# One-bank jobs freed of the other bank's readers, the last two density units in turn, and a density deadline five steps later

## The chip, the cores and the metric

The kernel runs on one core of a Trainium2 chip. The metric is device time in microseconds of one execution. Its engines run side by side, each through its own instructions in the order in which the program wrote them: TensorE (PE, with its weight loads PEld), VectorE (DVE), ScalarE (ACT), GpSimd (POOL) and SyncE (SP), which issues transfers here. They wait for each other on semaphores.

## What is computed

The input `x` is 8 images of 192 channels by 64 x 64 pixels, in fp32. Two layers follow each other, each with a group norm (32 groups) ahead of it and a residual around it:

```
x = x + attention(gn(x))      # q, k: 24 channels, v: 192; prelu on each
                              # softmax over 4096 x 4096 scores, times v
x = x + density(gn(x))        # per channel, per pixel: likelihood of a bin of width 1
```

The density evaluates a small network per channel at `x - 0.5` and at `x + 0.5`: layers of 1, 3, 3, 3, 1 numbers with positive weights, and after each of the first three layers `l + tanh(f) * tanh(l)`. Its value is the absolute difference of two sigmoids, at least 1e-6.

## The kernel before

The program is written out step by step by a planner in Python that runs while the program is built. An image's queries come in 8 blocks of 512. A block takes 16 steps (`STEPS`), so an image takes 128 (`IMG`), and the stream over 8 images has 1024 steps (`last`). In each step the main loop issues:

- the score matmuls of the step to come (`scores`, L701) into the two-bank PSUM tile `sc`, and its exp on ACT (L705);
- the max matmuls of a block that is `LEAD` = 22 steps ahead (`max_step`, L644) into the two-bank tile `mx`, which has one buffer, and the reduction of it on VectorE (L648). So the max matmul of a step waits until the reduction of the step before is through;
- 8 attention matmuls (`attend`, L716) into an accumulator in one of two PSUM tiles, `turns`, of two banks each. Blocks take the two tiles alternately;
- and `work_off`, for everything else.

`work_off` first issues what is due at the step (`run_due`), then starts at most one job (`start_job`), then density operations (`density_step`), then one POOL piece of an ending (`pool_step`).

**Jobs** use the PSUM tile that the attention isn't accumulating into (`misc`), one bank of it or both. They start only in steps 3 to 14 of a block. `guest` holds the step from which each bank may be given out again: a job with a hold of h started at step t keeps its banks until t + h + 1, and a one-bank job gets the first bank that is free. One-bank jobs are: the norm's (`norm_end`: two small matmuls L391 and L404, and their readers L396 and L409 on VectorE, hold 3), the weights' (`weights`: L477 and on, readers L496 and L501), the keys' (`keys`: L544, read by two Relus on ACT, L529) and a block's maximum (`max_end`: four transposes, "turn", L668, read by the add L673 on VectorE). Two-bank jobs are queries (L573), values (L601) and a block's finish (transposes L749, then residual L758 on VectorE). Dependencies are drawn by whole tile: a write to a tile waits for all earlier readers of the tile.

At the start of an image several things meet, which the text below calls the seam: the finish of the last image's last block (step 3), the second norm of that image (steps 6 to 12, with `root` on ACT and `fourth`, L422 to L438, on VectorE), a turn (step 10), and the end of the density of the image before that. When `fourth` has run, `density(b)` appends 12 units.

**Density units.** A unit is one of two shifts (s = 0, 1) of one channel group of half an image: 23 VectorE operations on 128 x 1024 numbers (L958) with scale, linear and tanh operations on ACT between them (L926, L935, L941, L951). Up to three units are worked on, the oldest first. An operation is issued if what it needs on another engine was issued in an earlier step and enough of the 17 SBUF buffers are free, while its engine has credit. VectorE's credit grows each step by an allowance worked out from the operations left:

```
left = sum(len(u.todo["DVE"]) for u in units if u.key[0] == units[0].key[0])
rate = left * COST["DVE"] / max(1, (units[0].key[0] + 2) * IMG + 10 - t) + OTHER
```

with a cost of 1.22 and `OTHER` 0.1; what `run_due` issues for others on VectorE is deducted. So the density of image b is spread from about step 12 of image b + 1 to step 10 of image b + 2. When both units of a pair are done, `ending` follows: sum, tanh, sign, difference and mask on POOL and ACT, then `size` (L1120) and `store` (L1124), which frees the image's `xc` buffer (three of them) after the last channel group. The fetch of the next image but one into `xc` waits for that, and the finish of its first block waits for the fetch.

**After the stream** (the tail) the allowance is 4.15 a step. What is left of image 6's density runs beside the last norm; then image 7's density runs alone, in 11 of its 12 units with a layer of sums on TensorE (L899, then tanh L907 and gate L917), and its endings on VectorE and ACT (`alone`, L1102 to L1112).

Of the kernel before, what the change touches and what calls it, by code (L numbers as in the profile page):

```python
# [17 lines left out]
def kernel(  # L18
# [288 lines left out]
        scratch.append(pair)  # L307
    ready = [0, 0]

    def start_job(t):  # L310
        p = t % STEPS
        for n, (rank, make, hold, banks, cols) in enumerate(jobs):
            if stream[0] and (p < 3 or p + max(hold, 1) >= STEPS):
                continue
            at_ = [i for i in range(2) if guest[i] <= t]
            if len(at_) < banks:
                if rank < 2:
                    return
                continue
            k = [i for i in (1, 0) if ready[i] <= t and scratch[i][0].shape[1] >= cols]  # L320
            if cols and not k:
                continue
            del jobs[n]
            pm = misc()
            for i in at_[:banks]:
                guest[i] = t + hold + 1
            if cols:
                ready[k[0]] = t + 2
            parts = make(pm if banks == 2 else pm[:, at_[0], :], scratch[k[0]] if cols else None)
            for i, fn, cost, act, pe in parts:  # L330
                at(t + i, fn, cost, act, pe)
            return
# [47 lines left out]
    def norm_end(key, n, t, then=None):  # L380
# [7 lines left out]

        def mean():
            pm = cell["pm"]  # L390
            nc.tensor.matmul(pm[:, 0:2], lhsT=gavg, rhs=cell["mv"], start=True, stop=True)  # L391

        def second():
            mv, pm = cell["mv"], cell["pm"]
            res = cell["res"] = small.tile([128, 2], F32, tag="nrm", bufs=4, name=f"nrm_{nm}")
            nc.vector.tensor_copy(res, pm[:, 0:2])  # L396
            dv = cell["dv"] = small.tile([128, 2], F32, tag="dv", name=f"dv_{nm}")
            nc.vector.tensor_tensor(dv[:, 0:1], mv[:, 0:1], res[:, 0:1], ALU.subtract)
            nc.vector.tensor_tensor(dv[:, 0:1], dv[:, 0:1], dv[:, 0:1], ALU.mult)
            nc.vector.tensor_copy(dv[:, 1:2], dv[:, 0:1])  # L400

        def variance():
            pm = cell["pm"]
            nc.tensor.matmul(pm[:, 2:4], lhsT=gavg, rhs=cell["dv"], start=True, stop=True)  # L404

        def third():
            res, pm = cell["res"], cell["pm"]
            ve = cell["ve"] = small.tile([128, 1], F32, tag="ve", name=f"ve_{nm}")
            nc.vector.tensor_tensor(ve, res[:, 1:2], pm[:, 2:3], ALU.add)  # L409
            nc.vector.tensor_scalar(ve, ve, 1e-5, None, ALU.add)  # L410
            at(now[0] + 1, root, 0.0, 2.8)
            at(now[0] + 2, fourth, 1.5)
# [33 lines left out]

        def make(pm, _):
            cell["pm"] = pm
            return [
                (0, mean, 0.0, 0.0, 0.4), (1, second, 0.8, 0.0, 0.0),  # L450
                (2, variance, 0.0, 0.0, 0.4), (3, third, 0.4, 0.0, 0.0),
            ]
# [7 lines left out]
    def weights(b, then):  # L460
        res = norms[b, 0]
        cell = {}

        def scale():
            for k, src, n in (("q", w1r, 2), ("k", w2r, 1), ("v", wa_sb, 1)):
                d = wf[k, b] = fold.tile(
                    [128, 3, src.shape[2]], F32, tag=f"w{k}", bufs=n, name=f"w{k}_{b}"
                )
                nc.scalar.activation(d, src, AF.Copy, scale=res[:, 1:2])
            mb = cell["mb"] = fold.tile([128, 128], F32, tag="mb", name=f"mb_{b}")  # L470
            nc.vector.tensor_copy(mb, res[:, 0:1].to_broadcast([128, 128]))

        def products():
            pf = cell["pf"]
            p = slice(0, R)
            for g in range(3):
                nc.tensor.matmul(  # L477
                    pf[:, 0:2], lhsT=wf["q", b][p, g, :], rhs=res[p, 0:2],
                    start=g == 0, stop=g == 2,
                )  # L480
            for g in range(3):
                nc.tensor.matmul(
                    pf[:, 2:4], lhsT=wf["k", b][:, g, :], rhs=res[:, 0:2],
                    start=g == 0, stop=g == 2,
                )
            for g in range(3):
                nc.tensor.matmul(
                    pf[:, 4 : 4 + C], lhsT=cell["mb"][p], rhs=wf["v", b][p, g, :],
                    start=g == 0, stop=g == 2,
                )  # L490

        def offsets():
            pf = cell["pf"]
            for k, src, at_, n in (("bq", bq, 0, 2), ("bk", bk, 2, 1)):
                d = wf[k, b] = fold.tile([128, 2], F32, tag=k, bufs=n, name=f"{k}_{b}")
                nc.vector.tensor_tensor(  # L496
                    d[:, 0:1], src[:, 0:1], pf[:, at_ : at_ + 1], ALU.subtract
                )
                nc.vector.tensor_scalar(d[:, 1:2], d[:, 0:1], -1.0, None, ALU.mult)
            d = wf["ba", b] = fold.tile([128, C], F32, tag="ba", name=f"ba_{b}")  # L500
            nc.vector.tensor_tensor(d, ba_row, pf[:, 4 : 4 + C], ALU.subtract)  # L501
            then()

        at(now[0] + 1, scale, 0.3, 2.0)
        def make(pf, _):
            cell["pf"] = pf
            return [(0, products, 0.0, 0.0, 2.0), (1, offsets, 1.0, 0.0, 0.0)]

        at(now[0] + 3, lambda: job(make, 1))
# [10 lines left out]

    made = set()

    def prelu(name, dst, src, bias, nslope, u):


        def first():
            for i, sign in enumerate((1.0, -1.0)):
                b_ = bias[:, i : i + 1] if bias is not None else 0.0
                nc.scalar.activation(u[i], src, AF.Relu, bias=b_, scale=sign)  # L529

        def last():
            nc.vector.scalar_tensor_tensor(dst, u[1], nslope, u[0], ALU.mult, ALU.add)
            made.add(name)

        return first, last

    def keys(b, d, what, done):
        t = xi[what, b, d]

        def make(pk, u):  # L540
            if b not in kt:
                kt[b] = kpool.tile([128, N // 4], F32, tag="k", name=f"k_{b}")
            for g in range(3):
                nc.tensor.matmul(  # L544
                    pk[:, 0:P], lhsT=wf["k", b][:, g, :], rhs=t[:, g, :],
                    start=g == 0, stop=g == 2,
                )
# [4 lines left out]
            first, last = prelu(  # L552
                ("k", b, d), kt[b][p, at_ : at_ + P], pk[p, 0:P], wf["bk", b][p], nslope[p, 1:2],
                [x[p, 0:P] for x in u],
            )
# [98 lines left out]
    def max_end(b, n):  # L654
# [10 lines left out]
        def turn():  # L665
            pt = cell["pt"]
            for t in range(4):
                nc.tensor.transpose(pt[:, t * 128 : (t + 1) * 128], nm[:, t, :], ident)  # L668

        def add():  # L670
            u = (n % 2) * 256
            q = qt[b, n // 2][:, :, u : u + 256]
            nc.vector.tensor_tensor(  # L673
                q, q, cell["pt"].rearrange("p (s t) -> p s t", s=2), ALU.add
            )
            made.add(("max", b, n))

        def make(pt, _):
            cell["pt"] = pt
            return [(0, turn, 0.0, 0.0, 0.8), (1, add, 0.7, 0.0, 0.0)]  # L680

        at(now[0], collect, 0.4)
# [140 lines left out]
    class Unit:  # L823
# [146 lines left out]
        def more(self, k):  # L970
# [6 lines left out]
            if (n, j) == (3, 2):  # L977
                for q in range(3):
                    self.give(("l", 2, q))
                b, c, g, s = self.key  # L980
                if s == 1:
                    ending(b, c, g)

        def need(self):
# [22 lines left out]
    def density_step(t, rate):  # L1007
        if units and t < last:

            left = sum(len(u.todo["DVE"]) for u in units if u.key[0] == units[0].key[0])  # L1010
            rate = left * COST["DVE"] / max(1, (units[0].key[0] + 2) * IMG + 10 - t) + OTHER
        credit["DVE"] = min(credit["DVE"] + rate, 2 * rate)
        act = ACT_RATE if t < last else rate
        credit["ACT"] = min(credit["ACT"] + act, act)
        credit["PE"] = min(credit["PE"] + rate, rate)
        for eng in ("ACT", "PE", "DVE"):
            for n in range(min(3, len(units))):
                units[n].step(eng, t, list(units)[:n])
        while units and not units[0].todo["DVE"]:
            units.popleft()  # L1020

    def density(b):
        if b == B - 1:
# [291 lines left out]
```

## Time and profile before

| what | us |
|---|---|
| median of 3 runs | 5038.0 (5033.52 to 5038.48) |
| the profiled execution, its time | 5034.38 |
| its span | 5032.6 |
| first score matmul of the stream | 162.65 |
| of its last step | 4674.92 |
| last VectorE operation of the kernel (L1124) | 5026.72 to 5027.95 |

All of what follows reads one profiled execution. Its time is 1.8 us above its span. The granted TensorE clock is 0.982 of full speed in the mean. "Busy" is the time in which an engine has an instruction in work; matmuls overlap each other and their weight loads, so the distance between like instructions of neighbouring steps says more than their busy time. In a waits view a row is: engine, waiting line, what released it, total us, times, longest. In a windows view a row is: stretch, its length, then busy us and instruction count of PE, PEld, DVE, ACT and POOL, the granted clock, DMA share and GB/s. In a timeline a row is: start, length, engine, line, operation, out and in; idle time before it and its releaser stand in brackets.

### The profile page before, as it was taken

The page shows a single profiled execution, that of the slowest core. Times are in us where ns is not written, and L with a number is a line of the kernel's source. Part 1 is how long each engine was busy: PE and PEld are TensorE (multiplying, and loading weights), DVE is VectorE, ACT ScalarE, POOL GpSimd, SP SyncE. Part 2 cuts the span into 40 slices and gives each one's busy share as a digit, 9 for nine tenths or more (in the row PEclk, how much of TensorE's full clock was granted, in tenths as well). Part 3 has the DMA queues.
Part 4 walks back from the last instruction along what each step waited for, and adds up shares of the span by engine and source line. Part 5 has one row for each costly group of instructions (what it writes and reads, how often), then busy time and mean ns, then how long its engine had stood idle before and what let it go on. Part 6 is the DMA issues. An engine that isn't in the chain of part 4 may idle for free.

```text
span 5032.6 us, 69853 instructions
## 1 busy us (share of the span) xinstructions
PE 4804.2 (95%) x29152; PEld 3531.2 (70%) x29152; DVE 4306.7 (86%) x4455; ACT 3204.3 (64%) x3710; POOL 510.7 (10%) x493
## 2 busy tenths in 40 slices
PE   4999999999999999999999999999999999999596
PEld 2677777777777777777777777777777777777342
DVE  3433338999899998999899998999899998999878
ACT  1233336777677766777677766677677776677765
POOL 0000000111111200120101110120111110120000
PEclk9999999999999999999999999999999999999798
DMA  2000011010111112001111112001110111000000
GB/s 54 26 16 10 20 28 30 21 37 24 35 30 30 28 34 46 18 22 39 33 33 28 27 34 49 18 18 41 37 33 22 33 27 25 11 10 17 9 9 17
DMA packets 111952, 135.48 MB, mean 27 GB/s; under 512 B 14738, under 2 KB 93076, under 8 KB 111636
## 3 DMA queue, kind: packets, MB, share of 16 engines
q1 hardware_dynamic: 105856, 130.58, 10.6%
q8 instruction: 228, 3.74, 0.3%
q10 hardware_dynamic: 5780, 0.44, 0.1%
q14 instruction: 88, 0.72, 0.1%
HBM read 105.82 MB, written 25.17 MB: 26 GB/s over the span
## 4 chain that ended last, share of the span: by engine, by line
PE 72%; DVE 23%; ACT 3%; issue 1%; DMA 1%; POOL 1%; ACTq 0%; POOLq 0%; DVEq 0%
PE b L716 42%; PE sc L701 16%; DVE d L958 15%; DVE rm L648 5%; PE b L601 3%; PE b L899 2%; PE mx L644 2%; PE b L573 2%; PE b L544 1%; PE sc_tail L899 1%; PE mx_tail L899 1%; DVE st L378 1%; PE b L749 1%; ACT d L951 1%; PE b L668 1%
## 5 line engine op out<-in xcount | busy, mean ns | idle before, releaser
L716 PEld LDWEIGHTS b<-v,e 128*128 128x128 f32 x16384 | 2660.0, 190 | 779.1 <-issue 779.1
L716 PE MATMUL b<-v,e 128*128 128x193 f32 x16384 | 2963.8, 335 | 0.0
L705 ACT ACTIVATE e<-sc 128x1024 f32<-128x1024 f32 x1024 | 1046.2, 1022 | 1412.9 <-PE mx L644 1349.0
L648 DVE TENSOR_REDUCE rm<-mx 128x1 f32<-128x1024 f32 x1024 | 1248.8, 1220 | 556.5 <-PE mx L644 552.3
L644 PE MATMUL mx<-k,q 24*128 24x512 f32 x4096 | 1164.5, 645 | 23.4 <-DVE rm L648 23.1
L701 PE MATMUL sc<-q,k 25*128 25x512 f32 x4096 | 1158.1, 642 | 4.2 <-ACT e L705 4.0
L958 DVE SCALAR_TENSOR_TENSOR d<-d,wsp,d 128x1024 f32<-128x1024 f32 x768 | 985.6, 1284 | 47.3 <-ACT d L951 35.2
L958 DVE SCALAR_TENSOR_TENSOR d<-d,lc,d 128x1024 f32<-128x1024 f32 x765 | 968.3, 1279 | 16.3 <-ACT d L935 3.3
L958 DVE SCALAR_TENSOR_TENSOR d<-d,tf,d 128x1024 f32<-128x1024 f32 x543 | 681.4, 1280 | 4.0 <-ACT d L941 3.9
L941 ACT ACTIVATE d<-d 128x1024 f32<-128x1024 f32 x543 | 570.1, 1055 | 72.2 <-DVE d L958 71.3
L701 PEld LDWEIGHTS sc<-q,k 25*128 25x128 f32 x4096 | 307.2, 183 | 237.3 <-issue 201.2
L1040 POOL MEMSET pause<- 128x1 f32 x240 | 23.7, 99 | 4079.3 <-DVE d L958 4079.3
L951 ACT ACTIVATE d<-d,cb,wsp 128x1024 f32<-128x1024 f32 x351 | 433.1, 1235 | 7.1 <-DVE d L958 5.6
L926 ACT ACTIVATE d<-xc,bn,wn 128x1024 f32<-128x1024 f32 x288 | 353.3, 1233 | 4.5 <-DVE bn L438 4.4
L644 PEld LDWEIGHTS mx<-k,q 24*128 24x128 f32 x4096 | 309.1, 184 | 64.5 <-DVE rm L648 60.2
L935 ACT ACTIVATE d<-xc,bn,wn 128x1024 f32<-128x1024 f32 x255 | 314.5, 1234 | 0.1
L1087 POOL TENSOR_TENSOR d<-d,d 128x512 f32<-128x512 f32 x80 | 168.2, 2102 | 0.1
L1075 POOL TENSOR_TENSOR d<-d,d 128x512 f32<-128x512 f32 x80 | 166.3, 2078 | 7.8 <-DVE d L958 7.1
L1095 POOL TENSOR_TENSOR d<-d,d 128x512 f32<-128x512 f32 x80 | 159.6, 1995 | 2.1 <-POOL pause L1040 0.3
L601 PE MATMUL b<-wv,xi 64*128 64x192 f32 x1344 | 139.5, 340 | 0.0
L601 PEld LDWEIGHTS b<-wv,xi 64*128 64x128 f32 x1344 | 106.5, 186 | 25.4 <-issue 23.8
L1079 ACT ACTIVATE d<-d 128x512 f32<-128x512 f32 x160 | 91.8, 623 | 32.9 <-POOL d L1075 26.0
(157 smaller groups left out, 2337.3 us busy)
## 6 DMA issues: line engine op xcount, KB each, us to landing
xi<-in_x_dram SPq DMA_DIRECT2D x392, 192.0 KB, 3.5
xc<-in_x_dram SPq DMA_DIRECT2D x64, 384.0 KB, 5.8
out_dram<-xc SPq DMA_DIRECT2D x96, 256.0 KB, 3.1
d<-in_x_dram SPq DMA_DIRECT2D x16, 192.0 KB, 3.6
d<-in_wat_dram ACTq DMA_DIRECT2D x2, 144.0 KB
cb<-in_den_b_dram ACTq DMA_DIRECT2D x6, 2.2 KB
ff<-in_den_f_dram ACTq DMA_DIRECT2D x6, 2.2 KB, 4.8
bq<-in_b_dram ACTq DMA_DIRECT2D x4, 0.1 KB
```

Of the source, the lines that this page charges most:

```text
L601: nc.tensor.matmul(pv[:, s, 0:C], lhsT=t[p, g, k * 128 : k * 128 + 128] if g < 3 else one_row[p], rhs=wf["v", b][p, g, :] if g < 3 else wf ...
L644: nc.tensor.matmul(sc[:, s, :], lhsT=tile_of(qt[b, n // 2], n, j)[r], rhs=kt[b][r, u : u + F], start=True, stop=True,)
L648: nc.vector.tensor_reduce(out=rowmax[b, n][:, j, k : k + 1], in_=sc, axis=AX.XY, op=ALU.max)
L701: nc.tensor.matmul(sc[:, s, :], lhsT=kt[b][r, k : k + 128], rhs=qt[b, n // 2][r, :, u : u + 256], start=True, stop=True,)
L705: return lambda: nc.scalar.activation(e, sc, AF.Exp)
L716: nc.tensor.matmul(a[:, j, 0 : C + 1], lhsT=e[:, s, j * 128 : j * 128 + 128], rhs=v[:, s, p % 4, :], start=p == 0 and s == 0 and j % 2 == ...
L899: nc.tensor.matmul(out[:, h, :], lhsT=diag[g][:, 3 * i + n - 1 if n else 9 + i, :], rhs=src[:, h * F : h * F + F], start=n == 0, stop=n == 3,)
L926: nc.scalar.activation(self.buf[k], self.src(), AF.Tanh, bias=bn[:, s, g, 0, i : i + 1], scale=wn[:, g, 0, i : i + 1],)
L935: nc.scalar.activation(self.buf[k], self.src(), AF.Identity, bias=bn[:, s, g, 1, i : i + 1], scale=wn[:, g, 1, i : i + 1],)
L941: nc.scalar.activation(self.buf[k], self.buf["l", k[1], k[2]], AF.Tanh)
L951: nc.scalar.activation(self.buf[k], self.buf["l", n - 1, 0], AF.Identity, bias=offset, scale=wsp[:, g, w : w + 1],)
L958: nc.vector.scalar_tensor_tensor(dst, src, factor, dst, ALU.mult, ALU.add)
```

## The change

It has three parts.

1. One-bank jobs name their PSUM accesses. A matmul that writes bank i of tile n declares that it doesn't depend on the group of readers of bank 1 - i of that tile; a reader of bank i joins the group of bank i. Two-bank jobs, and the attention, are as before. A write still waits for readers of its own bank and for two-bank readers.
2. When just two density units are left, each engine is offered first to the unit with more VectorE operations to do. Either unit of a pair may now end last, so `ending` is called by whichever does, and units leave the queue in any order.
3. The deadline of an image's density is step 15 of the image after next instead of step 10.

```diff
+    spot = [None]
+
+    def spotted():
+        n, i = spot[0]
+        def write(inst):
+            tc.declare_no_dep(inst.ins, group=f"turn{n}{1 - i}", reason="reads the other bank")
+        def read(inst):
+            tc.add_to_no_dep_group(f"turn{n}{i}", inst.ins)
+        return write, read
...
     def start_job(t):
...
+            spot[0] = (now[0] // STEPS + 1) % 2, at_[0]
             parts = make(pm if banks == 2 else pm[:, at_[0], :], scratch[k[0]] if cols else None)
...
     def norm_end(key, n, t, then=None):
...
-            nc.tensor.matmul(pm[:, 0:2], lhsT=gavg, rhs=cell["mv"], start=True, stop=True)
+            cell["write"](
+                nc.tensor.matmul(pm[:, 0:2], lhsT=gavg, rhs=cell["mv"], start=True, stop=True)
+            )
...
-            nc.vector.tensor_copy(res, pm[:, 0:2])
+            cell["read"](nc.vector.tensor_copy(res, pm[:, 0:2]))
...
         def make(pm, _):
             cell["pm"] = pm
+            cell["write"], cell["read"] = spotted()
...
# the same around the matmuls and readers of weights, keys (with prelu) and max_end
...
                 b, c, g, s = self.key
-                if s == 1:
+                if not any(u.key == (b, c, g, 1 - s) and u.todo["DVE"] for u in units):
                     ending(b, c, g)
...
-            rate = left * COST["DVE"] / max(1, (units[0].key[0] + 2) * IMG + 10 - t) + OTHER
+            rate = left * COST["DVE"] / max(1, (units[0].key[0] + 2) * IMG + 15 - t) + OTHER
...
         for eng in ("ACT", "PE", "DVE"):
-            for n in range(min(3, len(units))):
+            order = list(range(min(3, len(units))))
+            if len(units) == 2:
+                order.sort(key=lambda n: -len(units[n].todo["DVE"]))
+            for n in order:
                 units[n].step(eng, t, list(units)[:n])
-        while units and not units[0].todo["DVE"]:
-            units.popleft()
+        for u in [u for u in units if not u.todo["DVE"]]:
+            units.remove(u)
```

More of the change, by code (lines that the diff above doesn't have):

```diff
@@ L403, in variance @@
             pm = cell["pm"]
-            nc.tensor.matmul(pm[:, 2:4], lhsT=gavg, rhs=cell["dv"], start=True, stop=True)
+            cell["write"](
+                nc.tensor.matmul(pm[:, 2:4], lhsT=gavg, rhs=cell["dv"], start=True, stop=True)
+            )
         def third():
@@ L408, in third @@
             ve = cell["ve"] = small.tile([128, 1], F32, tag="ve", name=f"ve_{nm}")
-            nc.vector.tensor_tensor(ve, res[:, 1:2], pm[:, 2:3], ALU.add)
+            cell["read"](nc.vector.tensor_tensor(ve, res[:, 1:2], pm[:, 2:3], ALU.add))
             nc.vector.tensor_scalar(ve, ve, 1e-5, None, ALU.add)
@@ L476, in products @@
             for g in range(3):
-                nc.tensor.matmul(
+                cell["write"](nc.tensor.matmul(
                     pf[:, 0:2], lhsT=wf["q", b][p, g, :], rhs=res[p, 0:2],
                     start=g == 0, stop=g == 2,
-                )
+                ))
             for g in range(3):
-                nc.tensor.matmul(
+                cell["write"](nc.tensor.matmul(
                     pf[:, 2:4], lhsT=wf["k", b][:, g, :], rhs=res[:, 0:2],
                     start=g == 0, stop=g == 2,
-                )
+                ))
             for g in range(3):
-                nc.tensor.matmul(
+                cell["write"](nc.tensor.matmul(
                     pf[:, 4 : 4 + C], lhsT=cell["mb"][p], rhs=wf["v", b][p, g, :],
                     start=g == 0, stop=g == 2,
-                )
+                ))
         def offsets():
@@ L495, in offsets @@
                 d = wf[k, b] = fold.tile([128, 2], F32, tag=k, bufs=n, name=f"{k}_{b}")
-                nc.vector.tensor_tensor(
+                cell["read"](nc.vector.tensor_tensor(
                     d[:, 0:1], src[:, 0:1], pf[:, at_ : at_ + 1], ALU.subtract
-                )
+                ))
                 nc.vector.tensor_scalar(d[:, 1:2], d[:, 0:1], -1.0, None, ALU.mult)
             d = wf["ba", b] = fold.tile([128, C], F32, tag="ba", name=f"ba_{b}")
-            nc.vector.tensor_tensor(d, ba_row, pf[:, 4 : 4 + C], ALU.subtract)
+            cell["read"](nc.vector.tensor_tensor(d, ba_row, pf[:, 4 : 4 + C], ALU.subtract))
             then()
@@ L506, in make @@
             cell["pf"] = pf
+            cell["write"], cell["read"] = spotted()
             return [(0, products, 0.0, 0.0, 2.0), (1, offsets, 1.0, 0.0, 0.0)]
@@ L521, with prelu @@
     made = set()
-    def prelu(name, dst, src, bias, nslope, u):
+    def prelu(name, dst, src, bias, nslope, u, read=lambda inst: None):
         def first():
@@ L528, in first @@
                 b_ = bias[:, i : i + 1] if bias is not None else 0.0
-                nc.scalar.activation(u[i], src, AF.Relu, bias=b_, scale=sign)
+                read(nc.scalar.activation(u[i], src, AF.Relu, bias=b_, scale=sign))
         def last():
@@ L542, in make @@
                 kt[b] = kpool.tile([128, N // 4], F32, tag="k", name=f"k_{b}")
+            write, read = spotted()
             for g in range(3):
-                nc.tensor.matmul(
+                write(nc.tensor.matmul(
                     pk[:, 0:P], lhsT=wf["k", b][:, g, :], rhs=t[:, g, :],
                     start=g == 0, stop=g == 2,
-                )
+                ))
             done()
@@ L553, in make @@
                 ("k", b, d), kt[b][p, at_ : at_ + P], pk[p, 0:P], wf["bk", b][p], nslope[p, 1:2],
-                [x[p, 0:P] for x in u],
+                [x[p, 0:P] for x in u], read,
             )
@@ L667, in turn @@
             for t in range(4):
-                nc.tensor.transpose(pt[:, t * 128 : (t + 1) * 128], nm[:, t, :], ident)
+                cell["write"](
+                    nc.tensor.transpose(pt[:, t * 128 : (t + 1) * 128], nm[:, t, :], ident)
+                )
         def add():
@@ L672, in add @@
             q = qt[b, n // 2][:, :, u : u + 256]
-            nc.vector.tensor_tensor(
+            cell["read"](nc.vector.tensor_tensor(
                 q, q, cell["pt"].rearrange("p (s t) -> p s t", s=2), ALU.add
-            )
+            ))
             made.add(("max", b, n))
@@ L679, in make @@
             cell["pt"] = pt
+            cell["write"], cell["read"] = spotted()
             return [(0, turn, 0.0, 0.0, 0.8), (1, add, 0.7, 0.0, 0.0)]
```

## The prediction

> **What bounds it now.** I read the page's engine line, then the busy table cut at steps of one image, then the waits of the stream, then the timeline at the longest of them.
>
> ```profile
> PE 4804.2 (95%) x29152; PEld 3531.2 (70%) x29152; DVE 4306.7 (86%) x4455; ACT 3204.3 (64%) x3710; POOL 510.7 (10%) x493
> ```
>
> TensorE is nearly never idle and VectorE is close behind. A stage is an image: 128 steps. I take a step from one first score matmul (L701) to the next. In the timeline a step without a job is 3.88 us. Image 0, which has no density beside it, takes 555.3 us (162.65 to 717.99); images 3 to 6 take 573.5 each with about the same TensorE work, image 2 571.9, image 1 566.5. Summing 3.88 per step and each job's matmuls as they show where nothing waits (turn 0.4, keys 1.3, queries and values 1.5, weights 2.7, finish 0.7) gives 554.3 for an image: 19.2 us of every later image are waits and their after-effects. Image 3 by steps 0-8, 8-16, 16-24, 24-128 (length, then PE, PEld, DVE, ACT, POOL busy, PEclk, DMA):
>
> ```profile
> 1856.50:1889.70 33.20, 33.20 (x215) 24.93 (x214) 29.47 (x32) 15.99 (x21) 0.00 (x0) 1.00 0.24 63
> 1889.70:1928.70 39.00, 36.68 (x214) 27.66 (x213) 30.47 (x47) 23.37 (x27) 4.44 (x6) 0.91 0.15 41
> 1928.70:1963.29 34.59, 33.08 (x197) 24.40 (x196) 31.49 (x34) 27.41 (x30) 6.74 (x7) 1.00 0.25 55
> 1963.29:2430.00 466.71, 463.84 (x2964) 349.57 (x2963) 455.15 (x446) 336.76 (x391) 65.55 (x60) 1.00 0.11 26
> ```
>
> VectorE has slack only around the image's seam: 12.3 us of 72.2 in the first 16 steps, against 11.6 of 466.7 in the last 104. Both engines are bounds there. Waits of the stream, 740 to 4660 us:
>
> ```profile
> PEld mx L644 <- DVE rm L648: 42.1, 45, 2.3
> ...
> PE mx L644 <- DVE rm L648: 13.0, 18, 1.5
> ...
> PE b L544 <- DVE q L673: 12.0, 12, 2.7
> PE b L668 <- DVE ve L409: 11.6, 5, 2.3
> ```
>
> Two kinds: one-bank jobs behind a VectorE reader (keys L544, turn L668), and the max matmul behind its own reduction, since `mx` has one buffer. The turn's wait at the seam of image 3, with what surrounds it:
>
> ```profile
> 1903.65 2.47 DVE L958 SCALAR_TENSOR_TENSOR d<-d,tf,d 128x1024 f32<-128x1024 f32 x2
> ...
> 1906.04 1.21 DVE L648 TENSOR_REDUCE rm<-mx 128x1 f32<-128x1024 f32 x1
> ...
> 1907.64 0.14 DVE L409 TENSOR_TENSOR ve<-nrm,b 128x1 f32<-128x1 f32 x1
> ...
> 1907.83 1.11 PE L668 MATMUL b<-ident,negmax 128*128 128x128 f32 x4 [2.32 <-DVE ve L409]
> ...
> 1910.89 4.74 PE L716 MATMUL b<-v,e 128*128 128x193 f32 x16
> ```
>
> The wait is 2.32 us, but the next 16 attention matmuls take 4.74 instead of 2.88, and the page's granted clock falls to 0.82 and 0.61 in the two 6 us slices from 1904. The two steps together are 5.8 us too long.
>
> [...] so a wait's price is not its length. [...]
>
> **Part 1, the waits across banks.** The second norm's job takes bank 0 for four steps from step 7; the turn of step 10 gets bank 1, yet waits for `ve`, a reader of bank 0: crosswise. So are the keys jobs of steps 43 and 59 (bank 1, behind the add of a turn in bank 0). The turns of steps 26 and 42 follow two-bank jobs: they stay. What goes at most, by step distances: seam 5.8 in images 3 to 6 and 4.3 in image 2; keys 1.0 + 1.2 in images 2 to 6; in image 1 keys 4.4 + 0.2, 1.6 and 0.3; in image 7 1.3. Sum 23.2 + 4.3 + 11 + 6.5 + 1.3 = 46. It adds no instruction and no wait. Not all is won: next late is the max matmul. At the seam the reduction ended at 1907.25, while the turn could have run at 1905.45 and the scores at 1905.85; so 1.4 us of the 5.8 stays unless VectorE's work there changes, and it does.
>
> **Part 2, the deadline.** VectorE's allowance per step is (units' operations left x 1.22)/(steps left) + 0.1. At an image's start 276 x 1.22 = 337 us are spread over 126 steps (step 12 to 138) now and 131 then: 2.67 to 2.57, 0.1 us less per step. At the boundary 19 operations are left now (26 for image 6); by the same formula 9 more then. So 9 x 1.26 = 11 us of VectorE work per image leave the saturated stretch (step 16 on) for the seam. There VectorE has 60.0 us of work now, 71 then, against 66.4 of TensorE work (72.2 less 5.8). The seam becomes VectorE's: 71 to 72 us. I take its gain as 0.5; bounds: +5.8 (TensorE alone sets it) and -4 (11 + 60 + the 5 us that VectorE waits now for `mx`). From step 16 on, 501.3 us hold 13.4 of waits: keys 2.1, turns 1.9 that stay, the max matmul late 8.5 (3.3 at steps 18-19, 2.9 at 46-48, 1.6 at 87), rest 0.9. With 11 us less for VectorE I take two thirds of the 8.5, 5.6, and the keys' 2.1. Bounds: 2.1 lost again to the reduction, nothing won (0), or 10.6. Image by image: 0.5 + 5.6 + 2.1 = 8.2, times five: **41**. Image 1 has no earlier density in its seam: 6.5 of keys less 1.5 taken back, plus 2 of its 3.7 us at step 17: **7** (3 to 11). Image 7: its 14.8 us of waits are the same kind, 1.3 crosswise; I take **6** (0 to 11).
>
> What the longer density delays: the image's last store, thus its `xc` buffer, and so the fetch of the next `xc`, which the first finish waits for (now at step 24, after a norm job frees the banks). By the code's counts it comes at step 28 or 29; the last slot of that block is 30. On SP's queue the fetch then stands 4 steps, 16 us, later among loads and stores that land in 3 to 6 us; POOL, 10% busy, runs the ending's pieces that much later. I cost both at nothing, the finish of step 24 having 6 steps of room; if it missed the slot, the weights and keys behind it would slip a block.
>
> **Part 3, units in turn.** A lone unit alternates: two adds, then tanh L941 and scale L951 on ACT. The tail shows it:
>
> ```profile
> 5001.30 2.60 DVE L958 SCALAR_TENSOR_TENSOR d<-d,wsp,d 128x1024 f32<-128x1024 f32 x2
> ...
> 5006.16 2.60 DVE L958 SCALAR_TENSOR_TENSOR d<-d,wsp,d 128x1024 f32<-128x1024 f32 x2 [2.26 <-ACT d L951]
> ...
> 5011.07 2.61 DVE L958 SCALAR_TENSOR_TENSOR d<-d,wsp,d 128x1024 f32<-128x1024 f32 x2 [2.31 <-ACT d L951]
> ...
> 5026.72 1.23 DVE L1124 SCALAR_TENSOR_TENSOR xc<-d,xc 128x1024 f32<-128x1024 f32 x1 [1.12 <-ACT d L1120]
> ```
>
> The new test ahead of `ending` runs while the program is written and costs nothing. In the stream the turns only even out VectorE's bursts, counted in the seam. At the very end 4.6 us of holes can be filled by the other unit, but the last unit's own chain starts from its third product's tanh (4997.52), behind TensorE; it could start 1.5 us earlier. I take **1.5** (0 to 4.6). In the hand-over (4681.5 to 4722) two such holes, 1.54 and 1.61, go: **3**.
>
> **Part 4, the price.** At the last attention step 26 operations of image 6 were left and ran among the last norm's chain; the residual L758 came at 4698.84, though its transposes ended near 4689. Nine more at 1.26 put **11** us ahead of image 7's density; nothing covers them, since VectorE is busy there but for those holes. If the steps after the norm take some of them up, 5; if the chain is held up as well, 14.
>
> **Sum.** -41 - 7 - 6 - 3 - 1.5 + 11 = -47.5. The profiled execution is 5034.4 us (span 5032.6), 3.6 below the median of 5038.0. 5034.4 - 47.5 = 4987; I say **4988**.
>
> **Rivals.** *Conserved*: VectorE is 97 to 99% busy from step 24, so a wait taken from TensorE reappears as a late reduction. For it: the 45 waits of L644. Against: 11 us per image really leave that stretch. Then only some 2.5 of the seam's 5.8 and image 1's keys are won: 5 x 2.5 + 5 in the stream, 8 lost in the tail: 5025. Chance 0.15 (some of it within 0.2%). *Slower*: the overrun. If density until step 15 and the next image's first units (they start at step 12) both draw on VectorE, the seam needs 60 + 14 operations x 1.26 = 78 us, plus the 5 us it must still wait for `mx`: 83 against 72, so 5 x 11 = 55 lost at the seam; 5 x 7.7 = 38 won after it and 7 in image 1; 11 lost in the tail, 4 in image 7's seam: 5034 + 25 = 5059. It decides once a seam passes 72 + 7 = 79 us, where 5 x 7 + 15 eats the 45 won. Against: jobs' costs are deducted from the allowance. Chance 0.09. *It doesn't do what it says*: the waits of L668 and L544 stay for another reader; then parts 2 to 4 alone, 5 x 5.6 + 8 - 8 = 28 won: 5007. Chance 0.06. My forecast 0.70.
>
> **Numbers.** 0.2% (10 us) is about what a measurement can tell from no change. Faster: 0.70 + 0.06 + 0.08 of the first rival = 0.84; within 0.07; slower 0.09. The bounds above give 4960 at the low end; the high end takes in the conserved case: 5031.
>
> **What would show it.** L668 no longer waits for L409, nor L544 at steps 43 and 59 for L673; clock 1.00 at the seam; images 2 to 6 at 565 us, VectorE's busy time per image unchanged at 547 but 70 of it in the first 16 steps; the last attention step about 53 us earlier than 4675, and the time from there to the end about 6 us longer. Wrong: images still at 570 or more with longer waits of L644, or a tail longer by over 15.

## The result, and the profile after

| | before | after |
|---|---|---|
| median, us | 5038.2 (4 runs) | 5006.2 (4 runs, 5002.7 to 5010.1) |
| ratio, 95% interval | | 0.9937, 0.992 to 0.9954 |
| profiled execution, its span | 5034.4, 5032.6 | 5008.8, 5007.0 |

The change makes the kernel 32 us faster by the medians. The two profiled executions differ by only 25.7, since that of before lies 3.9 under its median and that of after 2.6 over it; the stages below are cut from these two and add up to 25.7.

| stage, us | before | after | difference | predicted |
|---|---|---|---|---|
| up to the first score matmul | 162.7 | 158.2 | -4.4 | 0 |
| image 0 | 555.3 | 555.3 | 0 | 0 |
| image 1 | 566.5 | 559.3 | -7.2 | -7 |
| images 2 to 6 | 2865.8 | 2847.8 | -18.1 | -41 |
| image 7, to its last step | 524.6 | 517.0 | -7.6 | -6 |
| tail | 357.7 | 369.3 | +11.6 | +6.5 |

The engine line of the page after:

```profile
PE 4790.3 (96%) x29152; PEld 3530.8 (71%) x29152; DVE 4315.7 (86%) x4455; ACT 3201.9 (64%) x3710; POOL 511.7 (10%) x493
```

The counts are those of before: the same instructions in another order. The waits of the stream of after, 740 to 4660 us (lines have moved: `max_step` is L668, its reduction L672, a block's four transposes L693, keys L568, scores L728, attention L743, density L985):

```profile
PEld mx L668 <- DVE rm L672: 37.3, 34, 2.3
...
PE mx L668 <- DVE rm L672: 14.6, 18, 1.5
```

No row with keys or transposes behind a VectorE reader is left, where before had 12.0 and 11.6 us of them. The max matmul waits for its reduction as much as before: 34 weight loads in place of 45, but longer ones, and TensorE itself 14.6 us in place of 13.0. Image 3 in the stretches 0-8, 8-16, 16-24, 24-128 of its steps (windows view):

```profile
1842.76:1875.97 33.21, 33.21 (x213) 24.94 (x211) 31.89 (x35) 21.44 (x28) 10.67 (x10) 1.00 0.19 53
1875.97:1909.75 33.78, 33.78 (x213) 25.90 (x212) 33.20 (x49) 26.65 (x27) 0.00 (x0) 1.00 0.17 48
1909.75:1945.20 35.45, 34.60 (x198) 25.95 (x197) 33.36 (x37) 24.89 (x31) 11.70 (x12) 0.95 0.00 0
1945.20:2413.81 468.61, 465.48 (x2961) 352.09 (x2960) 448.67 (x439) 330.17 (x384) 53.73 (x50) 0.99 0.13 31
```

The seam, the first two rows, went from 72.2 to 67.0 us, and its clock from 0.91 to 1.00. The third row grew by 0.9 and the fourth by 1.9, although VectorE has 6.5 us less to do in the fourth (448.7 for 455.2). Work left the saturated stretch and the stretch became longer: that is the thing to explain. The timeline of after shows it in image 2, where the queue reaches step 109:

```profile
1749.11 1.28 DVE L985 SCALAR_TENSOR_TENSOR d<-d,tf,d 128x1024 f32<-128x1024 f32 x1
...
1750.30 2.60 DVE L985 SCALAR_TENSOR_TENSOR d<-d,wsp,d 128x1024 f32<-128x1024 f32 x2
...
1752.82 2.48 DVE L985 SCALAR_TENSOR_TENSOR d<-d,lc,d 128x1024 f32<-128x1024 f32 x2
...
1755.21 1.22 DVE L672 TENSOR_REDUCE rm<-mx 128x1 f32<-128x1024 f32 x1
...
1756.48 1.95 PE L668 MATMUL mx<-k,q 24*128 24x512 f32 x4 [1.46 <-DVE rm L672]
...
1758.36 5.38 PE L743 MATMUL b<-v,e 128*128 128x193 f32 x16
```

Five density operations (1 + 2 + 2) stand in a row ahead of a reduction. It ends at 1756.43, the next max matmuls start 0.05 later, and TensorE has sat idle for 1.46 us. The 16 attention matmuls after it take 5.38 in place of 2.88. From score matmul to score matmul (1753.90 to 1763.68) the step takes 9.78 for 3.88: 5.9 us lost. In images 2 to 6 this place costs 5.9, 4.2, 2.6, 5.8 and 4.2, in all 22.7 us. Before has its bursts of five at steps 16 and 44 of each of these images, and what comes behind them costs 3.3 and 2.9 an image.

### The profile page after: what moved, and what is told of

Its sections match the earlier page's. It is cut to its first block, busy times and chain, and to the rows that moved or that the text cites. A ratio compares the mean times of both kernels' runs of the same rounds, so it can differ in the third digit from the quotient of the medians.

```text
span 5007.0 us, 69881 instructions
## 1 busy us (share of the span) xinstructions
PE 4790.3 (96%) x29152; PEld 3530.8 (71%) x29152; DVE 4315.7 (86%) x4455; ACT 3201.9 (64%) x3710; POOL 511.7 (10%) x493
## 4 chain that ended last, share of the span: by engine, by line
PE 83%; DVE 12%; ACT 3%; issue 1%; POOL 1%; DMA 0%; ACTq 0%; SPq 0%; DVEq 0%; POOLq 0%
PE b L743 50%; PE sc L728 19%; DVE d L985 7%; PE b L625 4%; DVE rm L672 3%; PE b L926 2%; PE b L597 2%; PE b L568 2%; PE mx L668 2%; PE sc_tail L926 1%; PE mx_tail L926 1%; PE b L776 1%; ACT d L968 1%; DVE st L394 1%; ACT d L978 1%
## 5 line engine op out<-in xcount | busy, mean ns | idle before, releaser
L743 PEld LDWEIGHTS b<-v,e 128*128 128x128 f32 x16384 | 2662.9, 191 | 778.6 <-issue 771.8
L743 PE MATMUL b<-v,e 128*128 128x193 f32 x16384 | 2966.8, 335 | 0.0
L672 DVE TENSOR_REDUCE rm<-mx 128x1 f32<-128x1024 f32 x1024 | 1248.8, 1220 | 528.5 <-PE mx L668 523.1
L668 PE MATMUL mx<-k,q 24*128 24x512 f32 x4096 | 1161.7, 643 | 24.8 <-DVE rm L672 24.7
L728 PE MATMUL sc<-q,k 25*128 25x512 f32 x4096 | 1154.2, 640 | 9.5 <-ACT e L732 9.5
L985 DVE SCALAR_TENSOR_TENSOR d<-d,wsp,d 128x1024 f32<-128x1024 f32 x768 | 984.2, 1283 | 45.0 <-ACT d L978 34.7
L985 DVE SCALAR_TENSOR_TENSOR d<-d,lc,d 128x1024 f32<-128x1024 f32 x765 | 979.6, 1289 | 19.3 <-ACT d L962 5.1
L985 DVE SCALAR_TENSOR_TENSOR d<-d,tf,d 128x1024 f32<-128x1024 f32 x543 | 680.8, 1276 | 2.7 <-ACT d L968 2.5
L728 PEld LDWEIGHTS sc<-q,k 25*128 25x128 f32 x4096 | 306.2, 183 | 242.0 <-issue 198.0
L668 PEld LDWEIGHTS mx<-k,q 24*128 24x128 f32 x4096 | 308.1, 184 | 60.4 <-DVE rm L672 54.8
L625 PEld LDWEIGHTS b<-wv,xi 64*128 64x128 f32 x1344 | 106.5, 186 | 25.4 <-issue 21.3
L926 PE MATMUL b<-d,v 128*128 128x512 f32 x204 | 94.5, 615 | 17.0 <-ACT d L953 17.0
```

Source lines behind the costliest of these rows:

```text
L625: nc.tensor.matmul(pv[:, s, 0:C], lhsT=t[p, g, k * 128 : k * 128 + 128] if g < 3 else one_row[p], rhs=wf["v", b][p, g, :] if g < 3 else wf ...
L668: nc.tensor.matmul(sc[:, s, :], lhsT=tile_of(qt[b, n // 2], n, j)[r], rhs=kt[b][r, u : u + F], start=True, stop=True,)
L672: nc.vector.tensor_reduce(out=rowmax[b, n][:, j, k : k + 1], in_=sc, axis=AX.XY, op=ALU.max)
L728: nc.tensor.matmul(sc[:, s, :], lhsT=kt[b][r, k : k + 128], rhs=qt[b, n // 2][r, :, u : u + 256], start=True, stop=True,)
L743: nc.tensor.matmul(a[:, j, 0 : C + 1], lhsT=e[:, s, j * 128 : j * 128 + 128], rhs=v[:, s, p % 4, :], start=p == 0 and s == 0 and j % 2 == ...
L926: nc.tensor.matmul(out[:, h, :], lhsT=diag[g][:, 3 * i + n - 1 if n else 9 + i, :], rhs=src[:, h * F : h * F + F], start=n == 0, stop=n == 3,)
```

## The experiments

The three edits are called banks, turn and deadline here: parts 1, 2 and 3 in the list of the change, while the prediction has the deadline as its part 2 and the turns as its part 3. The edit turn is not the "turn" of a block's maximum; that one is called the transposes below. The credit that `density_step` saves up for VectorE is capped at `2 * rate`, about 5.1 us in the stream; operations of 1.22 go out while it is above zero, so a step can issue five. A cap of 3.5 or 3.6 allows three. No experiment leaves out work. The ratio is to executions of before made together with the kernel's own; their median was 5036.4 to 5036.9 in the experiments, and what is said below to be gained against before is counted from these. "Waits of mx" below is the row of PEld L668 behind the reduction in the waits of images 1 to 7, and in brackets that of PE.

| kernel | median us | ratio to before (95%) | waits of mx |
|---|---|---|---|
| before | 5038.2 | | 42.1 (13.0) |
| banks | 5009.6 | 0.9952 (0.994 to 0.9964) | 47.5 (14.6) |
| turn | 5015.4 | 0.9958 (0.9946 to 0.9971) | 18.3 (7.9) |
| turn, deadline | 5030.7 | 0.9982 (0.9974 to 0.999) | 36.1 (14.2) |
| banks, deadline | 5058.6 | 1.0042 (1.003 to 1.0055) | 67.0 (37.6) |
| banks, turn | 4977.6 | 0.9882 (0.9867 to 0.9897) | 32.5 (10.0) |
| all three (after) | 5006.2 | 0.9937 (0.992 to 0.9954) | 37.3 (14.6) |
| all three, deadline not for image 6 | 5001.4 | 0.993 (0.9917 to 0.9942) | 39.3 (14.3) |
| all three, cap 3.5 | 4969.2 | 0.9869 (0.9854 to 0.9884) | 28.9 (8.3) |
| cap 3.6 alone | 5001.3 | 0.9929 (0.9916 to 0.9943) | 11.8 (none) |
| banks, cap 3.6 | 4983.8 | 0.9893 (0.988 to 0.9907) | 13.5 (none) |
| banks, turn, cap 3.6 | 4959.8 | 0.9846 (0.9833 to 0.9859) | 6.3 (none) |
| the same, and more credit at the end | 4951.7 | 0.9831 (0.9818 to 0.9845) | 6.6 (none) |

### e1: banks alone

Against after:

```diff
-            rate = left * COST["DVE"] / max(1, (units[0].key[0] + 2) * IMG + 15 - t) + OTHER
+            rate = left * COST["DVE"] / max(1, (units[0].key[0] + 2) * IMG + 10 - t) + OTHER
...
-            order = list(range(min(3, len(units))))
-            if len(units) == 2:
-                order.sort(key=lambda n: -len(units[n].todo["DVE"]))
-            for n in order:
+            for n in range(min(3, len(units))):
```

> Only part 1: one-bank jobs are freed, the deadline stays at step 10 and units go oldest first. Theory (the waits across banks, with the clock that they cost, are the gain; what VectorE still owes takes a part back): prologue 4 us less, image 1 about 7, images 2 to 6 about 4.4 at the seam and 1 to 2 at the keys each, image 7 about 1, tail unchanged: 40 us less than before, about 4998, that is as good as or better than the whole change (32 less). Rival (VectorE conserves: each wait comes back as a late reduction): the seam keeps over half of its 5.8, images 2 to 6 win 2 us each, 15 to 20 us less in all, 5020; the rest of the change's gain is then the deadline's.

Measured 5009.6, between the two. Image 1 gained 3.7 us, images 2 to 6 together 14.8, image 7 0.5; the tail was 357.6, as before. The rest of the 24.8 between the profiled executions, 5.7, is ahead of the first score matmul. The seam took 68.8. The transposes no longer wait there, and the waits view shows what came in their place:

```profile
PEld mx L668 <- DVE rm L672: 47.5, 51, 2.3
```

The row was 42.1 us, 45 times before. So the freed waits are real, and a part of them comes back as late reductions.

### e2: turn and deadline, without banks

Against after:

```diff
         def write(inst):
-            tc.declare_no_dep(inst.ins, group=f"turn{n}{1 - i}", reason="reads the other bank")
+            return inst
         def read(inst):
-            tc.add_to_no_dep_group(f"turn{n}{i}", inst.ins)
+            return inst
```

> Only parts 2 and 3: units in turn and the deadline at step 15; the dependencies are drawn by whole tile as before. Theory: the seam keeps the turn's wait and its slow clock (70 to 73 us for 16 steps), the keys keep theirs, images 2 to 6 end within 3 us of before, the tail is 11 us longer: 0 to 12 us slower than before, 5038 to 5050. Rival (the deadline moves VectorE work out of the saturated stretch and wins by itself): 10 to 28 us less than before, 5010 to 5028.

Measured 5030.7, some 6 us less than before: by this median a hit for neither. But the 18 executions lie between 5016.9 and 5040.9, in two groups: seven up to 5022.4 with a mean granted clock of 0.982 to 0.984, eleven from 5029.0 on with 0.979 to 0.981. No other kernel here spreads so far, and no run shows what puts an execution into one group or the other; the profiled one, 5035.1, is of the second. Its seam takes 67.0 us, as short as that of after, with the dependence across banks in place. The timeline of after says why:

```profile
1889.48 1.22 DVE L672 TENSOR_REDUCE rm<-mx 128x1 f32<-128x1024 f32 x1
...
1891.08 0.14 DVE L429 TENSOR_TENSOR ve<-nrm,b 128x1 f32<-128x1 f32 x1
...
1891.63 0.60 PE L693 MATMUL b<-ident,negmax 128*128 128x128 f32 x4
```

`ve`, the reader that the transposes of step 10 waited for, ends at 1891.22, before TensorE comes to them at 1891.63. In the new plan the norm's chain no longer stands behind a pair of density operations here, so the wait would not have been met anyway. Of the waits across banks only keys are left in e2, 8.6 us.

### e3: banks and turn, with the old deadline

Against after:

```diff
-            rate = left * COST["DVE"] / max(1, (units[0].key[0] + 2) * IMG + 15 - t) + OTHER
+            rate = left * COST["DVE"] / max(1, (units[0].key[0] + 2) * IMG + 10 - t) + OTHER
```

> Parts 1 and 2 without part 3: the deadline stays at step 10. Theory: the gain of part 1, and no work is pushed into the tail, so it loses the 11 us that the change pays there: 40 to 48 us less than before, 4990 to 4998, faster than the whole change by 8 to 16. Rival (the later deadline is what empties the seam of late reductions): the seam stays at 69 us or more in images 2 to 6, and the run is no faster than the whole change: 5006 or above.

Measured 4977.6, 59 less than before and 29 less than the whole change: the direction of the theory, and better than it. Images 2 to 6 took 2823.2 for after's 2847.8, the tail 356.3 for 369.3; image 7 was the longer one, 524.4 for 517.0, and image 1 562.9 for 559.3. The steps from 24 on of image 3 (windows view of e3), to be laid beside after's 468.61:

```profile
1939.87:2401.10 461.23, 461.06 (x2958) 349.08 (x2957) 450.48 (x446) 333.54 (x389) 64.99 (x60) 1.00 0.10 23
```

VectorE has 1.8 us more to do in it than in after, and it is 7.4 us shorter.

### e4: banks and deadline, oldest unit first

Against after:

```diff
-            order = list(range(min(3, len(units))))
-            if len(units) == 2:
-                order.sort(key=lambda n: -len(units[n].todo["DVE"]))
-            for n in order:
+            for n in range(min(3, len(units))):
```

> Parts 1 and 3 without part 2: units oldest first, with the deadline at step 15. The last unit of an image, alone and waiting for ACT every two operations, ends at step 17 and VectorE gets 5, 4 and 5 operations in steps 15 to 17. Theory (bursts of VectorE operations in one step make the max matmul late): steps 14 to 20 lose 4 to 8 us more per image than in the whole change, so 15 to 30 us slower than it, 5020 to 5035. Rival (the order of the last two units matters little in the stream): within 5 us of the whole change, 5001 to 5011.

Measured 5058.6: slower than before, beyond what the theory asked. The waits of its stream:

```profile
PEld mx L668 <- DVE rm L672: 67.0, 43, 5.5
...
PE mx L668 <- DVE rm L672: 37.6, 20, 4.7
```

The lone last unit gets 5, 4 and 5 density operations in steps 15 to 17, and steps 17 and 19 are 3.9 to 5.4 and 6.8 to 7.7 us too long. Without turn the deadline moves an image's end into a burst.

### e5: the whole change, with a cap of three operations a step

Against after:

```diff
-        credit["DVE"] = min(credit["DVE"] + rate, 2 * rate)
+        credit["DVE"] = min(credit["DVE"] + rate, 2 * rate if t >= last else 3.5)
```

> The whole change, and in the stream VectorE's credit is cut at 3.5, so that a step issues at most 3 density operations (the change has steps with 5 and 4 of them; 3.8 us of work more than the step can hold). Theory (what the change still loses in images 2 to 6 are bursts in one step that make the max matmul late, and the slow clock after it): the 2.6 to 5.9 us at step 109 and about half of the 3.1 at steps 87 and 88 go: 20 to 30 us less than the whole change, 4976 to 4986. Rival (VectorE's mean load makes the reductions late; spreading it only moves the lateness): within 6 us of the whole change, 5000 to 5012.

Measured 4969.2, 37 less than after and more than the 20 to 30 expected. Images 2 to 6 fall to 562.8 each. The place at step 109 of image 2 in the timeline of e5:

```profile
1741.84 2.60 DVE L985 SCALAR_TENSOR_TENSOR d<-d,wsp,d 128x1024 f32<-128x1024 f32 x2
...
1744.35 1.22 DVE L672 TENSOR_REDUCE rm<-mx 128x1 f32<-128x1024 f32 x1
...
1745.62 0.70 PE L668 MATMUL mx<-k,q 24*128 24x512 f32 x2
...
1746.68 2.88 PE L743 MATMUL b<-v,e 128*128 128x193 f32 x16
```

Three density operations (one stands just before these lines) instead of five, no bracket behind the max matmuls, and 2.88 us of attention. The place lost 22.7 us in images 2 to 6 of after and loses 1.1 an image in e5, so it accounts for 17.0 of the 33.8 us that these images won; the rest is a balance of other places. After lost 3.1 an image at steps 87 and 88 and 1.1 at 67 and 68. In steps 12 to 16, with at most three operations in a step, e5 still loses 5.9 an image, more than after; the account of the prediction below comes back to this.

### e6: the whole change, with the old deadline for image 6

Against after:

```diff
-            rate = left * COST["DVE"] / max(1, (units[0].key[0] + 2) * IMG + 15 - t) + OTHER
+            rate = left * COST["DVE"] / max(1, (units[0].key[0] + 2) * IMG + (15 if units[0].key[0] < B - 2 else 10) - t) + OTHER
```

> The whole change, but image 6's density keeps the deadline at step 10: 26 instead of 34 operations are left after the last step of the stream. Theory (each operation that is left lengthens the tail by 1.26 us, since VectorE sets the last norm's time there): tail from 369 back to 357 to 360, image 7 up to 7 us longer (its waits return to what they were): 2 to 10 us less than the whole change, about 5001. Rival (the last norm's chain of small steps sets the hand-over, not VectorE's queue): tail stays at 366 or more, and with image 7 longer the run is 5006 to 5013.

Measured 5001.4. The tail fell from 369.3 to 360.4 and image 7 rose from 517.0 to 523.5. What the deadline costs in the tail it gives back in image 7 to within 2 or 3 us, so the tail is not where the change loses.

### e7 and e8: banks and turn with the cap, then with more credit at the end

e7 against e3:

```diff
-        credit["DVE"] = min(credit["DVE"] + rate, 2 * rate)
+        credit["DVE"] = min(credit["DVE"] + rate, 2 * rate if t >= last else 3.6)
```

e8 against e7:

```diff
+            if t >= last - LEAD + 4:
+                rate += 1.0
-        credit["DVE"] = min(credit["DVE"] + rate, 2 * rate if t >= last else 3.6)
+        credit["DVE"] = min(credit["DVE"] + rate, 2 * rate if t >= last - LEAD + 4 else 3.6)
```

> Parts 1 and 2 with the deadline at step 10, and the credit cut at 3.6 in the stream (at most 3 operations in a step). Theory (bursts): the 2.4 us at step 17 and about half of the 3.2 at steps 44 to 53 go in images 1 to 6, the 3.7 at steps 17 and 86 of image 7 too: 15 to 25 us less than parts 1 and 2 alone (4977.6), 4953 to 4963. Rival (mean load): within 6 us of it, 4972 to 4984.

> As the run with parts 1 and 2 and the cut credit, and from 18 steps before the end of the stream, where no max reduction is left to do, VectorE's allowance is 1.0 us higher: 18 instead of 26 operations are left for the tail. Theory: tail 8 x 1.26 = 10 us shorter (346 instead of 356), the end of image 7 not longer since VectorE has idle time there: 8 to 11 us less than without it. Rival (the last norm's chain sets the hand-over): tail within 3 us of 356.

Measured 4959.8 and 4951.7, both as expected. In e7 the max matmul hardly waits any more (waits of its stream):

```profile
PEld mx L668 <- DVE rm L672: 6.3, 18, 0.5
```

and images 2 to 6 take 559.7 to 562.8, against 555.3 for image 0, which has no density beside it. With the cap the deadline costs 9.4 us (e5 against e7; the caps, 3.5 and 3.6, allow the same three operations) where it cost 28.6 without (after against e3). In the last 18 steps no max matmul is left to be delayed, so e8 lets VectorE work ahead there. Eight operations fewer are left at the end, and the hand-over (last score matmul at 4600.23) ends sooner, in the timeline of e8 and below it that of after, whose last score matmul is at 4637.71 (the reciprocal opens `fourth`, the last step of the last norm):

```profile
4638.63 0.15 DVE L442 RECIPROCAL rq<-sq 128x1 f32<-128x1 f32 x1
```

```profile
4694.54 0.16 DVE L442 RECIPROCAL rq<-sq 128x1 f32<-128x1 f32 x1
```

That is 38.4 against 56.8 us, and 47.4 in e7. e8 is the fastest kernel of the study, 85 us or 1.7% under before and 54 under after.

### e9: turn alone

Against before (who calls `ending`, and how units leave the queue, as in the change):

```diff
-            for n in range(min(3, len(units))):
+            order = list(range(min(3, len(units))))
+            if len(units) == 2:
+                order.sort(key=lambda n: -len(units[n].todo["DVE"]))
+            for n in order:
```

> Only part 2: units in turn; whole-tile dependencies and the deadline at step 10 as before. Asked: is the turn's gain its own, or does it need the free banks? It still issues 4 operations at step 9, so the transposes of step 10 should wait for the norm's reader as before. Theory (turns and banks work on the same lateness at the seam, and the keys' waits stay): seam 70 us or more, keys 2 us each image, 10 to 25 us less than before, 5012 to 5027, so that parts 1 and 2 together (4977.6, 59 less) win more than the sum of each alone (27 + 10 to 25). Rival (their gains add up): 32 us less, 5005.

Measured 5015.4, 21 less than before. The waits of its stream:

```profile
PE b L568 <- DVE q L699: 24.1, 12, 2.7
...
PEld mx L668 <- DVE rm L672: 18.3, 21, 1.8
...
PE b L693 <- DVE ve L429: 12.2, 5, 2.5
```

The max matmul waits less than half as long as before (18.3 for 42.1), while the waits across banks, which this kernel keeps, grow from 23.6 to 36.3. So turn works on the reduction and banks on the rest, and the two together (e3) win more than 27 + 21.

### e10 and e11: the cap alone, and with banks

e10 against before, e11 against e1:

```diff
-        credit["DVE"] = min(credit["DVE"] + rate, 2 * rate)
+        credit["DVE"] = min(credit["DVE"] + rate, 2 * rate if t >= last else 3.6)
```

> None of the change; only VectorE's credit in the stream is cut at 3.6 (at most 3 density operations in a step). Theory (bursts are the largest part of what images 2 to 6 lose): the 3.3 us at steps 18 and 19, the 2.9 at 46 to 48 and the 1.6 at 87 go, and the turn's wait at the seam shrinks: 30 to 45 us less than before, 4992 to 5007, as much as the whole change. Rival (the waits across banks are the larger part, and without them gone nothing moves): within 10 us of before.

> Part 1 with the credit cut at 3.6; units oldest first, deadline at step 10. With parts 1 and 2 and the cut it was 4959.8. Theory (the turn's 32 us on top of part 1 come from the bursts that the lone last unit leaves behind, so the cut does most of the turn's work): 4962 to 4972. Rival (the turn fills VectorE's holes at the seam, which the cut cannot): 4980 or more.

Measured 5001.3 and 4983.8, the second a miss for the theory and a hit for its rival. The cap alone wins 35 us, as much as the whole change, with an edit of one line; it takes the waits of mx from 42.1 to 11.8 us and those across banks from 23.6 to 13.0. Turn on top of banks and cap (e7 against e11) still wins 24: it is not only another way to cut the bursts. Nor is it mainly the seam, as the rival had it: there e7 is shorter by 0.9 to 2.6 us an image, 7.9 of the 25.3 that images 2 to 6 win between the two.

## Why the prediction was right, and where it was not

It said 4988, faster, with 4960 to 5031 as the range; 5006 lies inside, 18 us from the forecast. The range was wide, and there is luck in the hit: of 47.5 us in the sum, the stages that it priced show 21.3 in the profiled executions, and another 4.4 came ahead of the first score matmul, where nothing was forecast. Terms that were wrong stand on both sides of the sum.

**Part 1, the waits across banks: right in mechanism.** That TensorE can write one bank of a tile while VectorE reads the other was the author's assumption; the trace of after shows it: at step 43 of image 3 six keys matmuls (L568) run from 2039.75 to 2041.21, and the add L699, which reads the other bank, runs beside them, from 2040.27 to 2040.95. At the same step of before they started at 2058.15, when that add had ended at 2058.09. The waits are gone to the last, and the warning that a part comes back as a late reduction shows in e1: of the 46 us "at most", all within the images, 19 were won there with banks alone. Image 1 won 7.2 for 7, but not by the terms of the sum: the keys' 6.5 came whole, and step 17 costs its 3.7 as before, where 2 were to go. With banks alone image 1 won 3.7.

**Part 2, the seam: mis-sized.** Predicted 71 to 72 us with VectorE as its bound and 0.5 won; it takes 67.0 and won 5.2, near the upper bound of 5.8. VectorE's work there rose from 60.0 to 65.1, not to 71, and the transposes found nothing to wait for even without banks (e2). The counts of the plan were right: 28 operations left at the boundary, as worked out, and 34 for image 6 where 35 were expected. The fetch and the first finish fitted as expected, at step 28.

**Part 2, the steps from 16 on: this step failed.** "With 11 us less for VectorE I take two thirds of the 8.5, 5.6, and the keys' 2.1." In images 3 to 6 these steps take 504.1, 499.5, 502.3 and 504.0 against 501.3: nothing won, 1.2 lost in the mean, for 7.7 expected. The bound "nothing won (0)" named the case. The reasoning took it that less work for VectorE on the whole makes the reductions less late. Two places show what it left out.

The first is a burst. 0.1 us less allowance per step leaves the same cap of five operations, and only shifts the steps in which credit is spent. In images 2 to 6 of before, bursts fell on steps 16 and 44; in after, on step 107, and the step that pays for it, 109, loses 2.6 to 5.9 us. That e5 removes the burst, and the loss but for 1.1 us, shows the cause of this part. Which step a burst falls on was to be had from the planner's counts, before any run.

The second lies around the line between the seam and the rest, and no step there has more than three density operations. In image 3 of after, VectorE's only idle time over 0.15 us from 1873.3 to 1921.7 is one of 0.17. In step 16 the max matmul is late, in the timeline of after:

```profile
1914.89 1.22 DVE L672 TENSOR_REDUCE rm<-mx 128x1 f32<-128x1024 f32 x1
...
1916.17 1.22 PE L668 MATMUL mx<-k,q 24*128 24x512 f32 x4 [0.85 <-DVE rm L672]
...
1917.32 4.43 PE L743 MATMUL b<-v,e 128*128 128x193 f32 x16
```

Steps 12 to 16 of images 2 to 6 lose 18.8 us in after and 29.3 in e5, which has no bursts left; in before, e3 and e7, with the old deadline, they lose 1 us or less. So this part goes with the later deadline and with a VectorE that has no slack left there, not with bursts: "the seam becomes VectorE's" held, and the loss fell mostly just behind the seam's 16 steps. The sign that the text gave for being wrong, images still at 570 or more, was nearly there: they take 566.5 to 571.0. Image 7 won 7.6 for 6.

**The deadline as a whole has the wrong sign.** The prediction gave it 5 x 5.6 = 28 in images 2 to 6, less 11 in the tail. Four pairs of kernels show it as a loss: 49 with banks (e1, e4), 29 with banks and turn (e3, after), 15 with turn (e9, e2), 9 with banks, turn and cap (e7, e5). Taken from the first score matmul to the end of the profiled executions, which leaves out a stretch that moves on its own, it is 47, 25, 14 and 13. The pair with turn is the least sure by its medians, since e2 spreads over 24 us: e2's shortest execution, 5016.9, lies among e9's, which go from 5013.2 to 5018.1. With the deadline left out, the change gives 4978 (e3).

**Part 3, units in turn: mis-sized.** "In the stream the turns only even out VectorE's bursts, counted in the seam", and 4.5 us at the end. The stream was where it paid: turn is worth 21 alone, 32 with banks, 24 with banks and cap, most of it in images 2 to 6 (15.8 of the 19.9 us between the profiled executions of before and e9, 27.8 of 29.9 between e1 and e3). It does not make bursts of five rarer: before and e1 have 13 such steps in the stream, e9 and e3 have 14, while after, slower than e3, has 7. So the number of bursts doesn't rank the kernels, and by what path turn wins is not shown. Of the 4.5 at the end, the 3 of the hand-over came in part (2.3, see below) and the 1.5 did not show: from the reciprocal that opens the last norm's `fourth` to the end of the span it is 312.5 us after and 312.0 before. At the end of after, in the timeline, the second unit's holes are still there:

```profile
4985.49 2.61 DVE L985 SCALAR_TENSOR_TENSOR d<-d,wsp,d 128x1024 f32<-128x1024 f32 x2 [2.31 <-ACT d L978]
...
5001.14 1.23 DVE L1155 SCALAR_TENSOR_TENSOR xc<-d,xc 128x1024 f32<-128x1024 f32 x1 [1.12 <-ACT d L1151]
```

**Part 4, the price: right in kind, 2 us too small.** 11 us were expected for the operations left over, less the 3 that turn wins in the same stretch: 8. From the last score matmul to that reciprocal after takes 56.8 and before 45.7, 11.2 more. Turn alone shortens the stretch to 43.4 (e9, and e3 with banks), so the deadline costs 13.4 there, near the 14 that the text named should the norm's chain be held up as well. e8 shows the rate from the other side: eight fewer operations than e7, a tail 9.1 shorter.

**The rivals.** *Conserved* described the half of the truth that the forecast lacked (waits of mx 42.1 and 37.3), but its seam was wrong. *The overrun* did not come in its size: VectorE had 65 us in the seam, not 78; the loss of steps 12 to 16 is of its kind, 18.8 us where it put 55. e4 comes to its number, 5059, by another way, bursts of one lone unit. *It doesn't do what it says* is e2: 5031 where that rival gave 5007, because it counted on the same 28 us.

**What stays open.** The time up to the first score matmul lies between 150 and 164 us over these kernels, although the edits barely touch it; 4.4 us of the difference of the two profiled executions are there, and no run explains them; so differences of a few us between two kernels of the table carry that doubt. Why turn wins 24 even with bursts capped was not taken apart further, nor what parts the executions of e2.

## What to carry to other kernels

When two engines are both near their limit and hand work over through one buffer, count the burst as well as the mean: list how many operations of the filler work come out in each step, and ask in which steps they exceed the time that one hand-over allows. Try a limit on what a scheduler may save up before tuning its rate or its deadline; here one constant was worth 35 us alone. Ask of a later deadline where its work goes: here into a stretch in which VectorE then had no slack. And price edits in pairs: banks and turn won 27 and 21 alone, 59 together, and the deadline took back nearly half of it.

## What the runs showed of the hardware

A short idle time of TensorE cost a multiple of its length here, and not always the same one: the wait of 1.46 us at step 109 of after (1.45 in images 5 and 6) cost 5.9, 4.2, 2.6, 5.8 and 4.2 us in images 2 to 6. The granted clock accounts for the difference. The windows view of after, one row per image, with the clock third from the end:

```profile
1756.66:1763.48 6.82, 6.82 (x20) 5.21 (x20) 5.86 (x5) 2.95 (x3) 2.31 (x2) 0.50 0.00 0
2330.10:2333.51 3.41, 3.41 (x12) 3.11 (x11) 3.37 (x4) 0.68 (x1) 2.31 (x2) 0.50 0.00 0
2893.30:2903.54 10.24, 8.79 (x49) 5.99 (x49) 10.17 (x10) 6.19 (x7) 4.26 (x4) 1.00 0.00 1
3463.32:3470.15 6.83, 6.67 (x19) 5.17 (x19) 6.19 (x6) 2.95 (x3) 2.40 (x3) 0.50 0.00 0
4036.76:4040.17 3.41, 3.41 (x12) 2.69 (x9) 3.38 (x4) 0.46 (x1) 2.31 (x2) 0.50 0.01 2
```

The clock was 0.50 for 3.41 us in two images, for 6.82 or 6.83 in two and not at all in image 4, and each 3.41 us cost about 1.6 (2.6, 4.2, 5.8 to 5.9). The starts of the four stretches are 573.44, 1133.22 and 573.44 us apart, that is 168, 332 and 168 times 3.413. Waits of 1.45 or 1.46 us were thus followed by a clock of 0.50 in four images and by one of 1.00 in the fifth. What decides between the two, the runs don't show.
